# Two steps at a time in the first layer of a two-layer graph attention kernel: scores of both in a run, products of both in a run, the large unit behind

## The chip, the cores and the metric

The kernel runs on one core of one Trainium2 chip. A core has TensorE (matrix products, results into PSUM), VectorE, ScalarE and GpSimd (called POOL in the profile) for the rest, and SyncE (SP), which here only issues DMAs. Each engine takes its instructions strictly in the order in which the program issues them, and an instruction that waits holds up all that stand behind it on that engine. The metric is the device time of one execution, in microseconds, as the median of several runs.

## The reference

The input is 16 graphs of 1024 nodes with 256 features each, and a 0/1 adjacency matrix of 1024 x 1024 for each graph. Two layers follow one another. Each normalises its input, cuts it off at zero, and adds masked attention over the neighbours to the input. The first has 4 heads of 64, the second 8 heads of 32 with biases for q, k and v:

```python
h = jnp.maximum(_layernorm(x, axis=-1), 0.0)
x = x + _L0_gnn_ref(h, adj, Wq, Wk, Wv, Wo, bo)     # 4 heads of 64
h = jnp.maximum(_layernorm(x, axis=-1), 0.0)
x = x + _L1_gnn_ref(h, adj, Wq, bq, Wk, bk, Wv, bv, Wo, bo)   # 8 heads of 32

# inside a layer
scores = jnp.einsum('bhne,bhme->bhnm', Q, K) * scale
scores = jnp.where(mask, scores, -jnp.inf)
attn = jax.nn.softmax(scores, axis=-1)
heads = jnp.einsum('bhnm,bhme->bhne', attn, V)
out = concat(heads) @ Wo.T + bo
```

All of it is in fp32.

## The kernel before

The attention of the whole batch is one list of 768 **steps**. A step covers 512 queries (a half of the graph's rows) and four blocks of 128 keys x 512 queries. In layer 0 these are two heads times two key blocks, in layer 1 four heads times one key block. A **group** is the steps of one half and one set of heads: 4 steps in layer 0, 8 in layer 1. So a layer of one graph is 4 groups: 16 steps in layer 0, 32 in layer 1. The list starts with layer 0 of the first two graphs (32 steps), and then layer 1 of graph b and layer 0 of graph b+2 alternate, to the end.

For each step the program issues:

- **scores** (L447): four products of keys and queries into two PSUM buffers of the tag `ps_s`. There are three such buffers in all, each of two banks; the large units below use them too.
- **exponentials** (L463, L469): for each of the two buffers VectorE puts the mask on the scores, from PSUM into the SBUF tile p, and ScalarE takes the exponential in place. VectorE's L463 is what makes a score buffer free again.
- **weigh** (L481): the products with V, two steps later (`LEAD` is 2), into the PSUM tile po of the group, of which there is one.

The softmax's sums are column sums of p. In layer 0, `add_tiles` adds up a group's tiles (L490 on VectorE, L493 on POOL or VectorE, L494 and L496 on POOL), and `count_added` sums the result over the keys by a product with ones (L343). In layer 1 POOL adds pairs of tiles (L582), a DMA that accumulates adds those into one another (L568, issued by POOL), and `count` (L343) does the rest.

When a group has ended, a chain of small units follows at set distances, each entered in a table of due times by `later(i + k, f)` in `end_group` (L611): `copy_out` (L354, ScalarE, at once: it frees po), `spread` (ScalarE copy L362, then DMAs on SP that lay the sums over the partitions, L375, tile `sums`), `invert` (a reciprocal on VectorE, L383, and a DMA, L385), `fetch` (DMAs on SP, L393), `normalize` (POOL, L399), and for every second group `end_half`: the output product (L429), VectorE's addition to x (L434), and in layer 1 the DMAs to the output (L437).

Other due entries prepare coming layers: statistics (L191 to L201), normalisation (L210), turning of the normalised rows through DMAs (L236, L241, L248), the projections k, q (L266) and v (L302) with their copies out of PSUM (k: L274 or L280 on ScalarE; q: L272 or L278 on VectorE; v: L306 on ScalarE), bias (L219, POOL), the loading of x (L135, SP), the adjacency (L148, issued by POOL), its transpose by DMA (L154, SP) and its change into masks (L163, L171, ScalarE), and `test` (L288, VectorE), which checks the range of the sums.

The units `k`, `q`, `values` and `end_half` are called **large** (L25): they are long products on TensorE, each through one of the three score buffers. Within one step's due entries they are issued last (`rank`, L523). On an even step with a large unit the products with V are put off to the next step:

```python
if i % 2 or not self.large(i):
    for st in waiting:
        weigh(st)
```

So TensorE's order is "scores, products" step by step, or over two steps "scores, large unit, scores, products of two steps". All is issued by hand in this order (`manual_schedule`); the order of issue is the order of each queue.

In a layer-0 stage of 16 steps that begins at step a, the large units stand at a (k of layer 1), a+2 (q), a+4 (output of the layer-1 half before), a+8 (v) and a+12 (output of the other half).

Of the kernel before, what the change touches and what calls it, by code (L numbers as in the profile page):

```python
# [22 lines left out]
LEAD = 2  # L23
# [65 lines left out]
def fast_program(ctx, tc, a, w, loads, chk):  # L89
# [24 lines left out]
    def psum_pair(name):  # L114
        return ps_s.tile([P, 2, 512], F32, tag="ps_s", name=name)
# [323 lines left out]
    def scores(st):  # L439
        gr = st.gr  # L440
        D = gr.D
        st.ps = [psum_pair(f"ps_{st.n}_{i}") for i in range(2)]
        st.blocks = []
        for i in range(4):
            r, kt = (i, st.j) if gr.layer else (i % 2, 2 * st.j + i // 2)
            st.blocks.append((r, kt))
            nc.tensor.matmul(  # L447
                st.ps[i // 2][:, i % 2, :],
                gr.inp.kT[r * D : (r + 1) * D, gr.g, ts(kt, P)],
                gr.inp.qT[gr.qh][r * D : (r + 1) * D, gr.g, :],  # L450
                start=True, stop=True,
            )

    def exponentials(st, between):


        gr = st.gr
        odd = st.j % 2
        st.p = pp.tile([P, 4, 512], F32, tag=f"p{odd}", bufs=2 if odd else 7, name=f"p_{st.n}")
        for i in range(2):  # L460
            half = st.p[:, ts(i, 2), :]
            kt = st.blocks[2 * i][1]
            nc.vector.scalar_tensor_tensor(  # L463
                out=half,
                in0=gr.mask.m[gr.qh][:, kt, :].unsqueeze(1).to_broadcast([P, 2, 512]),
                scalar=-EDGE if gr.layer else BIG, in1=st.ps[i],
                op0=ALU.add if gr.layer else ALU.mult, op1=ALU.min,
            )
            nc.scalar.activation(half, half, AF.Exp, scale=gr.scale)  # L469
            if i == 0:  # L470
                for f in between:
                    f()

    def weigh(st):
        gr = st.gr
        D = gr.D
        if st.j == 0:
            gr.o = ps_o.tile([P, 512], F32, tag="po", name=f"po_{gr.n}")
        for i, (r, kt) in enumerate(st.blocks):
            h = gr.g * gr.per + r  # L480
            nc.tensor.matmul(  # L481
                gr.o[r * D : (r + 1) * D, :], gr.inp.v[:, kt, h * D : (h + 1) * D],
                st.p[:, i, :], start=(kt == 0), stop=(kt == NT - 1),
            )

    def add_tiles(one, two):


        a, b = one.p[:, 0:2, :], one.p[:, 2:4, :]
        nc.vector.tensor_add(a, a, b)  # L490

        engine = nc.vector if one.j else nc.gpsimd
        engine.tensor_add(b, two.p[:, 0:2, :], two.p[:, 2:4, :])  # L493
        nc.gpsimd.tensor_add(a, a, b)  # L494
        if one.j:
            nc.gpsimd.tensor_add(a, a, one.gr.t)  # L496
        one.gr.t = a

    def layer_steps(inp, mask):
        steps = []  # L500
        for qh in range(QH):
            half = Step()
            for g in range(2):
                steps += Group(inp, mask, qh, g, half).steps()
        return steps

    class Stream:
# [19 lines left out]
        def run(self):  # L527
            steps = self.steps
            n = len(steps)
            waiting = []  # L530
            for i in range(n + LEAD):
                now = steps[i] if i < n else None
                if i >= LEAD:
                    waiting.append(steps[i - LEAD])
                if now:
                    scores(now)
                copies = []
                if i % 2 or not self.large(i):
                    for st in waiting:
                        weigh(st)  # L540
                    for st in waiting:
                        if st.gr.layer:
                            self.count_steps(i, st)
                        if st.last:
                            copies.append(st.gr.copy_out)
                            self.end_group(i, st.gr)
                    waiting = []
                due = self.due.pop(i, [])

                for f, args in due:  # L550
                    if f.__name__ in COUNTS:
                        f(*args)
                if now:
                    exponentials(now, copies)
                else:
                    for f in copies:
                        f()
                if i % 2 and 3 <= i <= n and steps[i - 2].gr.layer == 0:
                    add_tiles(steps[i - 3], steps[i - 2])
                for f, args in sorted(due, key=self.rank):  # L560
                    if f.__name__ not in COUNTS:
                        f(*args)
            while self.due:
                for f, args in self.due.pop(min(self.due)):
                    f(*args)
# [140 lines left out]
    steps = layer_steps(inputs[0][0], masks[0])  # L706
# [37 lines left out]
    for t in range(NT):  # L744
        i = 5 + 2 * t
# [8 lines left out]
    for b in range(B - 1):  # L754
# [32 lines left out]
        else:  # L787
            last, e = inputs[1][b + 1], c + 32
# [256 lines left out]
```

## Time and profile before

| what | before |
|---|---|
| median of 3 runs | 3203.17 us (3202.34 to 3205.19) |
| the profiled execution | 3201.31 us |
| its span, first to last instruction | 3199.5 us |
| granted TensorE clock, mean | 0.997 |
| busy: TensorE / VectorE / ScalarE / POOL | 99% / 79% / 70% / 74% |
| layer-0 stage, 1113.76 to 1192.89 us | 79.13 us: TensorE 79.13, VectorE 63.99, ScalarE 51.06, POOL 53.28 busy |
| layer-1 stage, 1192.89 to 1309.13 us | 116.24 us: TensorE 115.91, VectorE 95.09, ScalarE 88.33, POOL 94.69 busy |
| opening 32 layer-0 steps, 37.90 to 206.76 us | 168.86 us: TensorE 165.86 busy |

A line of the timeline gives the start in us, the duration, the engine, the line of the kernel, the operation with its tiles and shapes, and how many records were merged. TensorE's fp32 products have two records each: x8 is one step's four products, x16 two steps'. Ends of products are modelled, so lengths are better read from one start to the next. A line of waits gives who waited for whom, the total in us, how often, and the longest. `[x <-who]` behind a timeline line is idle time of that engine just before it, and who ended it. SP and the queues of DMAs are listed as issues: the transfer ends later.

### The profile page before, as it was taken

Reading aid. Unit: us, or ns where it says so; the run is one execution under the profiler, and the core shown is the slowest. Engines: PE = TensorE matmul, PEld = TensorE weight load, DVE = VectorE, ACT = ScalarE, POOL = GpSimd, SP = SyncE. Lnnn points to the kernel's source line nnn. Section 1 sums busy time; section 2 is a strip of 40 time slices with the busy share of each in tenths; the row PEclk is TensorE's granted clock in tenths of the full one; section 3 lists DMA queues with packets and bytes.
Section 4 is the critical chain, followed back from the end, with each engine's and each line's share of the span. In section 5 each row is a group of like instructions: output and inputs, shape, how many; then the busy total and the mean of one; then the engine's idle time right before and its main releaser. Section 6 shows DMA issues by size and latency. Waiting matters only on the chain.

```text
span 3199.5 us, 44432 instructions
## 1 busy us (share of the span) xinstructions
PE 3153.7 (99%) x16662; PEld 1212.4 (38%) x16662; DVE 2532.5 (79%) x2786; ACT 2242.4 (70%) x2472; POOL 2352.4 (74%) x1103
## 2 busy tenths in 40 slices
PE   8999999999999999999999999999999999999998
PEld 3443433433334333333433334343343333333332
DVE  5677787887878888787887878878788887887776
ACT  5667677776767767677676776767777676775765
POOL 4567677786877868678686776877778687786776
PEclk9999999999999999999999999999999999999999
DMA  6326556364563645646465463655636456462321
GB/s 132 53 47 131 108 112 130 88 135 106 111 134 92 130 104 109 131 99 129 95 127 117 101 134 92 131 104 112 135 88 133 108 111 135 91 131 62 85 62 32
DMA packets 347792, 341.21 MB, mean 107 GB/s; under 512 B 196016, under 2 KB 290480, under 8 KB 330544
## 3 DMA queue, kind: packets, MB, share of 16 engines
q0 software_dynamic: 37584, 173.03, 29.2%
q1 hardware_dynamic: 309984, 165.26, 21.5%
q8 instruction: 133, 2.18, 0.3%
q14 instruction: 91, 0.75, 0.1%
HBM read 149.95 MB, written 47.96 MB: 62 GB/s over the span
## 4 chain that ended last, share of the span: by engine, by line
PE 89%; ACT 4%; DVE 3%; POOL 2%; issue 1%; DMA 1%; SPq 0%; DVEq 0%; POOLq 0%; ACTq 0%
PE ps L447 31%; PE po L481 27%; PE pq L266 13%; PE py L429 7%; PE pv L302 6%; PE pz L343 5%; DVE p L463 2%; ACT p L469 2%; ACT hn L210 1%; ACT mask L163 1%; POOL p L582 1%; POOL rstd L199 0%; ACT v L306 0%; DVE st L191 0%; DMA hT<-turned 0%
## 5 line engine op out<-in xcount | busy, mean ns | idle before, releaser
L463 DVE SCALAR_TENSOR_TENSOR p<-mask,ps 128x1024 f32<-128x1024 fp8e5 x1536 | 1796.8, 1212 | 461.3 <-PE ps L447 423.6
L469 ACT ACTIVATE p<-p 128x1024 f32<-128x1024 f32 x1536 | 1609.4, 1056 | 784.9 <-DVE p L463 745.4
L582 POOL TENSOR_TENSOR p<-p,p 128x2048 f32<-128x2048 f32 x255 | 1171.3, 4596 | 250.0 <-PE po L481 152.3
L447 PE MATMUL ps<-qT,kT 32*128 32x512 f32 (+1 forms) x6144 | 1134.1, 631 | 7.2 <-ACT v L306 4.4
L481 PE MATMUL po<-p,v 128*32 128x512 f32 (+1 forms) x6144 | 990.6, 601 | 2.1 <-ACT cat L354 1.8
L447 PEld LDWEIGHTS ps<-qT,kT 32*128 32x128 f32 (+1 forms) x6144 | 363.7, 184 | 706.2 <-issue 308.6
L494 POOL TENSOR_TENSOR p<-p 128x1024 f32<-128x1024 f32 x128 | 301.9, 2358 | 284.0 <-DVE p L493 275.3
L481 PEld LDWEIGHTS po<-p,v 128*32 128x32 f32 (+1 forms) x6144 | 229.2, 118 | 690.8 <-issue 500.3
L493 POOL TENSOR_TENSOR p<-p 128x1024 f32<-128x1024 f32 x64 | 150.8, 2357 | 173.3 <-DVE p L490 101.5
L266 PE MATMUL pq<-hT,wk 128*128 128x512 f32 x512 | 242.8, 618 | 8.9 <-DMA hT<-turned 6.3
L302 PE MATMUL pv<-wv,hT 128*128 128x256 f32 x1024 | 237.8, 385 | 0.0
L266 PE MATMUL pq<-hT,wq 128*128 128x512 f32 x512 | 236.6, 605 | 0.0
L429 PE MATMUL py<-wo,cat 128*128 128x256 f32 x1008 | 235.5, 386 | 0.5 <-POOL cat L399 0.2
L302 PEld LDWEIGHTS pv<-wv,hT 128*128 128x128 f32 x1024 | 189.4, 190 | 70.5 <-DVE p L463 30.4
L429 PEld LDWEIGHTS py<-wo,cat 128*128 128x128 f32 x1008 | 185.6, 190 | 72.5 <-issue 31.4
L343 PE MATMUL pz<-p,ones 128*32 128x512 f32 (+1 forms) x1248 | 196.1, 595 | 0.8 <-ACT s L362 0.8
L399 POOL TENSOR_TENSOR cat<-cat,inv 128x512 f32<-128x512 f32 x127 | 185.4, 1460 | 5.0 <-DMA inv<-vd 3.1
L219 POOL TENSOR_TENSOR x<-x,bo 128x1024 f32<-128x1024 f32 x64 | 152.1, 2376 | 15.8 <-DMA bo<-in_bo_dram 15.8
L490 DVE TENSOR_TENSOR p<-p 128x1024 f32<-128x1024 f32 x128 | 163.2, 1275 | 0.0
L210 ACT ACTIVATE hn<-x,shift,rstd 128x256 f32<-128x256 f32 x256 | 138.2, 588 | 24.9 <-DMA turned<-hn 17.7
L496 POOL TENSOR_TENSOR p<-p,p 128x1024 f32<-128x1024 f32 x64 | 151.5, 2367 | 5.0
L266 PEld LDWEIGHTS pq<-hT,wk 128*128 128x128 f32 x512 | 94.4, 194 | 153.3 <-issue 112.9
(51 smaller groups left out, 1665.4 us busy)
## 6 DMA issues: line engine op xcount, KB each, us to landing
p<-p POOLq DMA_DIRECT2D x133, 1024.0 KB, 7.7
adj<-in_adj_dram POOLq DMA_DIRECT2D x128, 256.0 KB, 4.2
turned<-hn SPq DMA_DIRECT2D x58, 512.0 KB, 2.9
hT<-turned SPq DMA_DIRECT2D x232, 128.0 KB, 3.1
x<-in_x_dram SPq DMA_DIRECT2D x128, 128.0 KB, 2.7
inv<-vd SPq DMA_DIRECT2D x128, 128.0 KB, 2.9
inv<-vd SPq DMA_DIRECT2D x252, 64.0 KB, 3.6
out_dram<-x SPq DMA_DIRECT2D x124, 128.0 KB, 2.4
```

The lines of the kernel that those rows point to most:

```text
L210: nc.scalar.activation(hn[:, ts(i, E)] if whole else self.blocks(half)[:, :, i, :], rows if whole else rows.rearrange("p (c q) -> p c q", ...
L266: nc.tensor.matmul(pq[:, m, :], wt[self.layer][:, c, ts(m, P)], self.hT[half][:, c, :], start=(c == 0), stop=(c == 1),)
L302: nc.tensor.matmul(pv[:, i, :], self.hT[half][:, c, ts(i, P)], w.v[self.layer][:, c, :], start=(c == 0), stop=(c == 1),)
L343: nc.tensor.matmul(self.s[r * self.D : (r + 1) * self.D, :], w.ones.to_broadcast([P, self.D]), p[:, r, :], start=start, stop=stop,)
L399: nc.gpsimd.tensor_mul(o, o, self.inv)
L429: nc.tensor.matmul(py[:, i, :], self.half.cat[:, c, ts(i, P)], w.o[self.layer][:, c, :], start=(c == 0), stop=(c == 1),)
L447: nc.tensor.matmul(st.ps[i // 2][:, i % 2, :], gr.inp.kT[r * D : (r + 1) * D, gr.g, ts(kt, P)], gr.inp.qT[gr.qh][r * D : (r + 1) * D, gr.g ...
L463: nc.vector.scalar_tensor_tensor(out=half, in0=gr.mask.m[gr.qh][:, kt, :].unsqueeze(1).to_broadcast([P, 2, 512]), scalar=-EDGE if gr.layer ...
L469: nc.scalar.activation(half, half, AF.Exp, scale=gr.scale)
L481: nc.tensor.matmul(gr.o[r * D : (r + 1) * D, :], gr.inp.v[:, kt, h * D : (h + 1) * D], st.p[:, i, :], start=(kt == 0), stop=(kt == NT - 1),)
L494: nc.gpsimd.tensor_add(a, a, b)
L582: nc.gpsimd.tensor_add(one, one, st.p)
```

## The change

The loop over steps takes two steps at once where the first belongs to layer 0, and one as before where it belongs to layer 1. For a pair (i, i+1) of layer 0 the order of issue is now: the scores of both steps; the products with V of steps i-2 and i-1, without putting off; sums that are due at i or i+1; the exponentials of both steps, with the copy of a finished group behind the first half of the first; `add_tiles`; and then the due entries of i and after them those of i+1, each set with its large units last. No due time is changed, and no instruction is added or left out; only the order differs. Since the layer-0 stages begin at even steps, the pairs are (a, a+1), (a+2, a+3) and so on.

```diff
-            waiting = []
-            for i in range(n + LEAD):
-                now = steps[i] if i < n else None
-                if i >= LEAD:
-                    waiting.append(steps[i - LEAD])
-                if now:
-                    scores(now)
+            waiting, i = [], 0
+            while i < n + LEAD:
+                wide = 2 if i < n and steps[i].gr.layer == 0 else 1
+                span = range(i, i + wide)
+                now = [steps[k] for k in span if k < n]
+                waiting += [(k, steps[k - LEAD]) for k in span if k >= LEAD]
+                for st in now:
+                    scores(st)
                 copies = []
-                if i % 2 or not self.large(i):
-                    for st in waiting:
+                if wide == 2 or i % 2 or not self.large(i):
+                    for _, st in waiting:
                         weigh(st)
-                    for st in waiting:
+                    for k, st in waiting:
                         if st.gr.layer:
-                            self.count_steps(i, st)
+                            self.count_steps(k, st)
                         if st.last:
                             copies.append(st.gr.copy_out)
-                            self.end_group(i, st.gr)
+                            self.end_group(k, st.gr)
                     waiting = []
-                due = self.due.pop(i, [])
+                due = [e for k in span for e in sorted(self.due.pop(k, []), key=self.rank)]
 
                 for f, args in due:
                     if f.__name__ in COUNTS:
                         f(*args)
-                if now:
-                    exponentials(now, copies)
-                else:
-                    for f in copies:
-                        f()
-                if i % 2 and 3 <= i <= n and steps[i - 2].gr.layer == 0:
-                    add_tiles(steps[i - 3], steps[i - 2])
-                for f, args in sorted(due, key=self.rank):
+                for st in now:
+                    exponentials(st, copies)
+                    copies = []
+                for f in copies:
+                    f()
+                for k in span:
+                    if k % 2 and 3 <= k <= n and steps[k - 2].gr.layer == 0:
+                        add_tiles(steps[k - 3], steps[k - 2])
+                for f, args in due:
                     if f.__name__ not in COUNTS:
                         f(*args)
+                i += wide
```

## The prediction

> **What bounds the kernel now.** I read the page first: its busy shares, then the chain that ended last.
>
> ```profile
> PE 3153.7 (99%) x16662; PEld 1212.4 (38%) x16662; DVE 2532.5 (79%) x2786; ACT 2242.4 (70%) x2472; POOL 2352.4 (74%) x1103
> PE 89%; ACT 4%; DVE 3%; POOL 2%; issue 1%; DMA 1%; SPq 0%; DVEq 0%; POOLq 0%; ACTq 0%
> ```
>
> TensorE is busy in 99% of the span and is 89% of the chain. The list of TensorE's waits holds 39 us in all, mostly at the two ends; in the middle it waits for nobody:
>
> ```profile
> PE ps L447 <- DVE p L463: 0.9, 4, 0.3
> PE pz L343 <- ACT s L362: 0.8, 1, 0.8
> ```
>
> So anything that shortens TensorE's stream shortens the span, and any wait put in front of it lengthens the span one for one. Next the timeline of one layer-0 stage of 16 steps, 1113.76 to 1192.89 (79.13 us). There are 14 such stages after the opening 32 layer-0 steps. TensorE, then the other queues:
>
> ```profile
> 1130.55 3.65 PE L481 MATMUL po<-p,v 128*64 128x512 f32 x16
> 1134.13 1.99 PE L447 MATMUL ps<-qT,kT 64*128 64x512 f32 x8
> 1136.05 3.72 PE L429 MATMUL py<-wo,cat 128*128 128x256 f32 x16
> 1139.70 1.99 PE L447 MATMUL ps<-qT,kT 64*128 64x512 f32 x8
> ...
> 1148.11 1.94 PE L481 MATMUL po<-p,v 128*64 128x512 f32 x8
> 1149.98 1.99 PE L447 MATMUL ps<-qT,kT 64*128 64x512 f32 x8
> ```
> ```profile
> 1128.20 0.83 POOL L568 DMA_DIRECT2D p<-p  x1
> 1133.78 2.34 POOL L493 TENSOR_TENSOR p<-p 128x1024 f32<-128x1024 f32 x1 [4.75 <-DVE p L490]
> 1136.20 2.37 POOL L494 TENSOR_TENSOR p<-p 128x1024 f32<-128x1024 f32 x1
> ```
> ```profile
> 1141.06 1.85 SPq L437 DMA_DIRECT2D out_dram<-x  x4
> 1145.03 1.75 SPq L135 DMA_DIRECT2D x<-in_x_dram  x4
> 1146.83 1.28 SPq L154 DMA_TRANSPOSE adjT<-adj  x1
> 1148.15 2.55 SPq L375 DMA_DIRECT2D sums<-s  x4
> ```
>
> A step's products alone take 1149.98 - 1148.11 = 1.87, two steps' in a run 1134.13 - 1130.55 = 3.58, so a turn out of the products costs 2 x 1.87 - 3.58 = 0.15. A step's scores take 1.92 to the next start; their four rounds are 0.43 apart in the trace, so a turn out of the scores costs about 0.20. A large unit with the turn behind it takes 3.63 to 3.65.
>
> **The gain.** Call the stage's steps a to a+15 and the pairs p0 to p7. The large units stand at a (K), a+2 (Q), a+4 (output), a+8 (V), a+12 (output). Their five pairs ran scores, unit, scores, products of two steps; now scores of two steps, products, unit: one turn out of scores fewer, 0.20 each. The three other pairs lose a turn of each kind, 0.35. Together 5 x 0.20 + 3 x 0.35 = 2.05 us a stage; by the same count about 4 in the opening.
>
> **PSUM.** There are three score buffers, and a run of two steps wants four: its last waits until the first mask operation (L463) has ended. With VectorE free that starts 1.18 after the run and takes 1.21, done at 2.44 with 0.05 to the wake-up; the last quarter is due at 2.68. So VectorE may come 0.23 late at no cost. Anything later stalls TensorE one for one plus 0.1. Before, products or a unit stood between, and the trace has L463 starting up to 2 to 3 us late (1152.97 against 1149.98) with no stall. This cover goes.
>
> I followed all queues through one stage with the durations of its rows. Most lateness is covered: VectorE's 4 x 1.13 for masks plus 1.2 or 2.5 of additions fits in a pair of 7.22; L288's waits behind POOL fall under a longer wait below; the Q copy and the output's addition end at 1.4 and 1.25 after the run's start. Five places aren't covered.
>
> (1) **p0, 0.55.** The copy of the finished group (L354) stands on ScalarE behind the first exponential and now waits for products at 5.6 after the pair's start. Three exponentials (0.96 apart), the mask step (1.04) and K's copies (1.3) follow, ending at 11.35; K's buffer is due at 9.12 + 1.82 = 10.94. Ends: 0 if ScalarE overlaps better, 0.9 if not.
>
> (2) **p2, 2.55.** The accumulating DMA L568 due at a+2 now stands on POOL behind the additions L493 and L494 of that pair, which wait for VectorE. With p1's products at time 0: L490 ends at 2.8, L493, L494 and L399 take 2.36 + 2.36 + 1.27 with their gaps, L568 is issued at 9.1 and lands 7.7 later (6.9 to 9.9 over all) at 16.8. The count that reads it (L343, due a+5) comes at 3.58 + 3.63 + 3.64 + 3.48 = 14.33. Ends 1.7 and 4.7; before, 17 us lay between issue and count.
>
> (3) **p4, 4.0.** SP works in order: after the output's addition of a+4 it issues output, x, transpose and then `sums`. By the rows above the last `sums` lands 12.2 after that addition began (1139.81, to 1150.12 + 1.9). The reciprocal L383 due at a+7 reads them. Before, from unit's end to reciprocal were 16.7 us (1139.70 to 1156.37). Now the unit ends directly at p3, which has no unit and lasts 7.22; VectorE reaches the reciprocal about 7.2 into it and is held until 12.3. Behind it stand p4's masks. The first starts at 12.5, 5.3 after p4's start instead of at most 1.41: 3.9 plus 0.1. Ends 3.5 and 4.5.
>
> (4) **p6, 2.1.** The mask load L148 of a+8 is now behind POOL's additions: issued 1.6 after p5's start. From L148 to `sums` landed were 8.8 (1162.60 to 1169.52 + 1.9; the transpose stands between). So the reciprocal of a+11 runs at 10.4, and p6's first mask 3.4 after its start. Ends 1.5 and 2.7.
>
> (5) **Start of layer 1, 3.3.** As (3), with the output of a+12 and the reciprocal of a+15: `sums` landed 13.65 after the addition here (1180.45 to 1192.21 + 1.9), so the first layer-1 mask starts 11 to 14 after p7's start; the second score step behind K, due at 11.9, waits for two masks. Ends 1.8 and 4.1.
>
> **Moved at no cost.** POOL: L399 of a+2, a+7 and a+10 follow the additions too, but the output units that read them come 5.8, 25 and 4 us after; L148 of a+4 lands by 3 into p3 and its transpose is needed in p4; L219 has only later layers waiting. ScalarE: the normalisation of a+13 waits for L199 and L201, now behind two additions, and pushes p7's exponentials back by some 4 us; their products follow only at a+17, 13 us after the scores. SP: place (L248) and fetch (L393) slip by up to 10 us behind `sums`, and their readers stand a stage and a pair later. Without these covers each would cost what it slips. p's buffers: the tightest, the odd step's second one, is free 0.4 before its mask.
>
> **The clock.** After TensorE's idle times of 4.13 and 2.17 us the granted clock was 0.51, and K took longer than its 3.70:
>
> ```profile
> 249.33 5.95 PE L266 MATMUL pq<-hT,wk 128*128 128x512 f32 x8 [4.13 <-DMA hT<-turned]
> ```
> ```profile
> 3008.49 4.93 PE L266 MATMUL pq<-hT,wk 128*128 128x512 f32 x7 [2.17 <-DMA hT<-turned]
> ```
> ```profile
> 3008.40:3011.80 3.40, 3.31 (x4) 1.51 (x5) 2.29 (x7) 2.99 (x3) 2.55 (x3) 0.51 0.38 77
> ```
>
> 3.4 us at half speed cost 1.7. Waits (2) to (5) are of this size, but a slow stretch after (3) only eats into (4). I take 1.0 a stage, ends 0 and 3.4, as not every gap need do it. The Trainium skill ("TensorE: Matmul & The Clock Gate", section "HAM oscillation — how this bites in real kernels") asks only that no gap exceed about 3.4 us. By that rule only (3) would slow the clock, (4) would take it up, and the sum would be 13 lower; the row with 2.17 speaks against so lenient a reading.
>
> **Sum.** A standard stage: -2.05 + 0.55 + 2.55 + 4.0 + 2.1 + 3.3 + 1.0 = +11.45; 13 of them (the ones that load x and masks for a later element): +149. The last layer-0 stage has no such loads: -2.05 + 0.55 + 2.55 + 0.3 = +1. The opening: -4, plus some 2 for a transpose that now waits for normalisation behind four exponentials, plus three groups with (4)'s wait: about +4. Together +154. The profiled execution ran 3201.31 (span 3199.5, 1.8 outside) and the median of three is 3203.17; I add to the median: about 3357.
>
> **Rivals.** *The turns saved and nothing else*: 14 x 2.05 + 4 = 33 off, 3170. For it: TensorE waits for nobody now, and all engines but it are at 70 to 79%. It decides where the waits add up to less than 2.05 a stage; against it, (3) alone is 4.0, with a slack of 16.7 needed 12.2. *Only (1) and (2) come true*, the sums landing in time: -2.05 + 0.55 + 2.55 = +1.05 a stage, 3217. For it: the reciprocal's waits for `sums` add up to only 7.5 us now; against it, one of those (0.41 before 1194.18) is the place of (5), so it has no slack even today. *The clock as the new bound*: each gap of 2 us or more halves it and nothing absorbs it: up to 18 a stage with all upper ends, 3420 to 3440. *It cancels out*: gain and waits within 0.2%, if pairs with units hide (3) and (5).
>
> **How the numbers follow.** The five waits with the turns: 0.72, its own range 3295 to 3415 (all lower ends together give 6.5 a stage, 3288; all upper ends are the clock rival). Only (1) and (2): 0.11. Turns alone: 0.07. Clock: 0.07. Cancelling: 0.03. The range goes down to 3212, which takes in the second rival, and up to 3415. A measurement of this kernel tells about 0.2%, 6.4 us; faster 0.07, same 0.03, slower 0.90.
>
> **What the profile after would show.** The gain: TensorE's timeline with L447 x16 and L481 x16, 3.64 and 3.58 to the next start. (2): TensorE's L343 waiting for the DMA p<-p some 14 times by about 2.5. (3) to (5): VectorE's L383 waiting for `sums`, 7.5 us grown to 100 to 170, and TensorE's L447 waiting for L463, 0.9 grown to some 120. (1): L447 waiting for the K copy L280 by about half a microsecond. Clock: granted TensorE clock below 0.99. The prediction is wrong if layer-0 stages come out at 77 us and TensorE's list of waits stays short; it is wrong in its parts if TensorE waits for ScalarE or the key projections instead.

## The result and the profile after

The change makes the kernel slower: 3395.99 us (3375.64 to 3401.86) against 3203.28 us (3202.34 to 3205.19). The ratio is 1.059, with a 95% interval of 1.0543 to 1.0636. The profile below is of an execution of 3401.86 us, with a span of 3400.0 and a mean granted clock of 0.974. In it the lines after L565 have moved down by three: the accumulating DMA is L571, and POOL's addition of layer 1 is L585.

The page of the kernel after, its busy shares and the chain that ended last:

```profile
PE 3224.3 (95%) x16662; PEld 1246.3 (37%) x16662; DVE 2495.0 (73%) x2786; ACT 2215.5 (65%) x2472; POOL 2349.9 (69%) x1103
PE 64%; ACT 10%; DVE 8%; DMA 6%; POOL 5%; issue 4%; SPq 2%; DVEq 0%; ACTq 0%; POOLq 0%
```

TensorE has fallen from 89% of the chain to 64%. No single engine took its place; what it lost is spread over ScalarE, VectorE, DMAs and POOL. Its busy time grew by 71 us although it runs the same 16662 products: that is mostly work at half clock. From the mean clocks, (1 - 0.974) x 3400 = 88 us are lost now and (1 - 0.997) x 3199.5 = 10 were lost before, so the clock alone accounts for some 78 of the 200 us (an estimate from the two means).

The list of waits, TensorE's first, then one line of VectorE's and one of ScalarE's (total us, how often, longest):

```profile
PE ps L447 <- DVE p L463: 83.5, 39, 4.9
PE pz L343 <- DMA p<-p: 34.0, 14, 3.5
PE py L429 <- POOL cat L399: 5.4, 11, 0.5
PE ps L447 <- ACT kT L280: 3.5, 15, 0.8
```
```profile
DVE vn L383 <- DMA sums<-s: 150.4, 33, 6.3
```
```profile
ACT cat L354 <- PE py L429: 313.6, 30, 13.6
```

The first two were 0.9 us and absent before, and the reciprocal's wait for the sums grew from 7.5 us to 150.4. The last line is new and large, and the prediction did not have it.

Stage by stage, each from its first scores to those of the next (mean over the 13 layer-0 stages of the middle, the layer-1 stage after each, and the time in each for which the granted clock was 0.5, called half clock here):

| | before | after | half clock, after |
|---|---|---|---|
| opening | 168.85 | 184.50 | 10.2 |
| layer-0 stage | 79.14 | 87.44 | 5.78 |
| layer-1 stage | 116.12 | 121.64 | 5.78 |
| last layer-0 stage | 79.4 | 84.0 | 3.4 |

13 x (8.30 + 5.52) + 15.65 + 4.6 = 199.9 of the 200.5 us by which the span grew. Of a round's 13.8 us (one stage of each layer), TensorE's idle times grew by 8.6 and half of 11.55 us at half clock is 5.78; with the gain of 2.05 off, 12.3. The other 1.5 show when TensorE's runs are read from one start to the next, against the kernel with every queue mended (at the end of the experiments). In the round below, five runs of layer 0 are longer by 0.07 to 0.27 us each than their idle time and the clock explain, and the stalled score step of layer 1 by some 0.8: the second half of its scores waited for L463 once more, which shows in the weight loads alone, since the modelled ends of the first half cover it (`PEld` is TensorE's weight load):

```profile
1067.59 0.50 PEld L447 LDWEIGHTS ps<-qT,kT 32*128 32x128 f32 x4 [0.83 <-DVE p L463]
```

One layer-0 stage of TensorE's timeline, 973.55 to 1059.73 (86.18 us), with what follows; the rows between are left out where nothing waits:

```profile
973.55 3.70 PE L447 MATMUL ps<-qT,kT 64*128 64x512 f32 x16
...
984.85 1.99 PE L447 MATMUL ps<-qT,kT 64*128 64x512 f32 x8 [0.20 <-ACT kT L280]
986.77 3.65 PE L481 MATMUL po<-p,v 128*64 128x512 f32 x16
990.36 3.70 PE L266 MATMUL pq<-hT,wq 128*128 128x512 f32 x8
993.99 3.83 PE L447 MATMUL ps<-qT,kT 64*128 64x512 f32 x16
...
1003.70 1.06 PE L343 MATMUL pz<-p,ones 128*32 128x512 f32 x8 [2.30 <-DMA p<-p]
...
1021.93 1.52 PE L447 MATMUL ps<-qT,kT 64*128 64x512 f32 x4 [3.52 <-DVE p L463]
1023.38 4.91 PE L481 MATMUL po<-p,v 128*64 128x512 f32 x16
...
1049.22 3.29 PE L429 MATMUL py<-wo,cat 128*128 128x256 f32 x14 [0.49 <-POOL cat L399]
...
1066.46 3.21 PE L447 MATMUL ps<-qT,kT 32*128 32x512 f32 x8 [1.96 <-DVE p L463]
1069.59 5.70 PE L481 MATMUL po<-p,v 128*64 128x512 f32 x16
```

The runs x16 are there: 3.63 to 3.64 us for two steps' scores to the next start, 3.59 for two steps' products. So are the waits, one after another. The two products of 4.91 and 5.70 us are 3.65 us elsewhere; they are what a slow clock costs. Windows of the same stage (start and end, then the busy times of five engines, the granted clock, DMA share and GB/s):

```profile
1003.70:1007.10 3.40, 3.40 (x19) 2.30 (x20) 0.00 (x0) 0.00 (x0) 3.32 (x2) 1.00 0.02 5
1021.93:1025.30 3.37, 3.37 (x10) 0.99 (x12) 3.33 (x3) 1.04 (x1) 1.92 (x2) 0.59 0.32 85
1066.46:1071.50 5.04, 5.04 (x14) 1.47 (x16) 4.94 (x8) 3.70 (x5) 1.61 (x1) 0.55 0.41 156
```

After the gap of 2.30 us the clock stayed full. After those of 3.52 and 1.96 it halved, and after the shorter of the two for longer; the last section says what goes with it.

Why the longest wait is there is read from SP's queue and VectorE's, of the kernel after:

```profile
1009.71 2.04 SPq L437 DMA_DIRECT2D out_dram<-x  x4
1013.68 1.75 SPq L135 DMA_DIRECT2D x<-in_x_dram  x4
1015.48 1.28 SPq L154 DMA_TRANSPOSE adjT<-adj  x1
1016.80 2.49 SPq L375 DMA_DIRECT2D sums<-s  x4
```
```profile
1008.45 1.23 DVE L434 TENSOR_TENSOR x<-py,x 128x1024 f32<-128x1024 f32 x1 [5.94 <-PE py L429]
...
1020.54 0.25 DVE L383 RECIPROCAL vn<-sums 128x16 f32<-128x16 f32 x1 [4.88 <-DMA sums<-s]
1020.72 4.55 DVE L463 SCALAR_TENSOR_TENSOR p<-mask,ps 128x1024 f32<-128x1024 fp8e5 x4
```

`sums` is the fourth in line on SP behind output, x and transpose; the reciprocal gets it 12.1 us after the output's addition began, and the masks for which TensorE waits stand behind the reciprocal.

### The profile page after: what moved, and what is told of

Read it like the earlier page. It is cut to its first block, busy times and chain, and to the rows that moved or that the text cites. A ratio compares the mean times of both kernels' runs of the same rounds, so it can differ in the third digit from the quotient of the medians.

```text
span 3400.0 us, 44449 instructions
## 1 busy us (share of the span) xinstructions
PE 3224.3 (95%) x16662; PEld 1246.3 (37%) x16662; DVE 2495.0 (73%) x2786; ACT 2215.5 (65%) x2472; POOL 2349.9 (69%) x1103
## 4 chain that ended last, share of the span: by engine, by line
PE 64%; ACT 10%; DVE 8%; DMA 6%; POOL 5%; issue 4%; SPq 2%; DVEq 0%; ACTq 0%; POOLq 0%
PE ps L447 20%; PE po L481 18%; PE pq L266 9%; PE py L429 7%; DVE p L463 6%; ACT p L469 6%; PE pv L302 5%; PE pz L343 5%; DMA p<-p 3%; DMA sums<-s 2%; POOL p L493 2%; ACT hn L210 1%; POOL cat L399 1%; ACT mask L163 1%; DVE p L490 1%
## 5 line engine op out<-in xcount | busy, mean ns | idle before, releaser
L463 DVE SCALAR_TENSOR_TENSOR p<-mask,ps 128x1024 f32<-128x1024 fp8e5 x1536 | 1786.9, 1213 | 439.4 <-PE ps L447 401.9
L469 ACT ACTIVATE p<-p 128x1024 f32<-128x1024 f32 x1536 | 1586.9, 1055 | 619.9 <-DVE p L463 585.7
L585 POOL TENSOR_TENSOR p<-p,p 128x2048 f32<-128x2048 f32 x255 | 1174.3, 4608 | 237.3 <-PE po L481 141.6
L447 PE MATMUL ps<-qT,kT 32*128 32x512 f32 (+1 forms) x6144 | 1148.2, 638 | 94.1 <-DVE p L463 83.5
L481 PE MATMUL po<-p,v 128*32 128x512 f32 (+1 forms) x6144 | 1022.3, 615 | 2.1 <-ACT cat L354 1.8
L447 PEld LDWEIGHTS ps<-qT,kT 32*128 32x128 f32 (+1 forms) x6144 | 375.8, 185 | 783.2 <-DVE p L463 320.6
L481 PEld LDWEIGHTS po<-p,v 128*32 128x32 f32 (+1 forms) x6144 | 243.6, 121 | 728.6 <-issue 502.6
L494 POOL TENSOR_TENSOR p<-p 128x1024 f32<-128x1024 f32 x128 | 301.1, 2352 | 300.7 <-DVE p L493 295.7
L354 ACT COPY cat<-po 128x512 f32<-128x512 f32 x128 | 74.0, 578 | 480.3 <-PE py L429 313.6
L429 PE MATMUL py<-wo,cat 128*128 128x256 f32 x1008 | 246.8, 398 | 5.6 <-POOL cat L399 5.4
L343 PE MATMUL pz<-p,ones 128*32 128x512 f32 (+1 forms) x1248 | 197.2, 599 | 34.8 <-DMA p<-p 34.0
L429 PEld LDWEIGHTS py<-wo,cat 128*128 128x128 f32 x1008 | 193.1, 197 | 84.5 <-issue 32.1
L399 POOL TENSOR_TENSOR cat<-cat,inv 128x512 f32<-128x512 f32 x127 | 184.0, 1449 | 5.4 <-DMA inv<-vd 3.6
L219 POOL TENSOR_TENSOR x<-x,bo 128x1024 f32<-128x1024 f32 x64 | 155.0, 2422 | 15.7 <-DMA bo<-in_bo_dram 15.6
L434 DVE TENSOR_TENSOR x<-py,x 128x1024 f32<-128x1024 f32 x63 | 76.9, 1220 | 121.2 <-PE py L429 120.0
L571 POOL DMA_DIRECT2D p<-p x133 | 118.0, 888 | 54.5 <-POOL p L585 31.4
```

The source lines that it names most:

```text
L343: nc.tensor.matmul(self.s[r * self.D : (r + 1) * self.D, :], w.ones.to_broadcast([P, self.D]), p[:, r, :], start=start, stop=stop,)
L399: nc.gpsimd.tensor_mul(o, o, self.inv)
L429: nc.tensor.matmul(py[:, i, :], self.half.cat[:, c, ts(i, P)], w.o[self.layer][:, c, :], start=(c == 0), stop=(c == 1),)
L447: nc.tensor.matmul(st.ps[i // 2][:, i % 2, :], gr.inp.kT[r * D : (r + 1) * D, gr.g, ts(kt, P)], gr.inp.qT[gr.qh][r * D : (r + 1) * D, gr.g ...
L463: nc.vector.scalar_tensor_tensor(out=half, in0=gr.mask.m[gr.qh][:, kt, :].unsqueeze(1).to_broadcast([P, 2, 512]), scalar=-EDGE if gr.layer ...
L481: nc.tensor.matmul(gr.o[r * D : (r + 1) * D, :], gr.inp.v[:, kt, h * D : (h + 1) * D], st.p[:, i, :], start=(kt == 0), stop=(kt == NT - 1),)
```

## The experiments

The theory is that of the prediction: the two runs gain about 2 us a stage, and what the order puts behind POOL's additions and behind SP's other DMAs costs more, through TensorE's waits and then the clock. The first rival is that the runs themselves are what costs, since three score buffers are too few for them. The second is that the clock, and not the waits, takes most.

**The accumulating DMA first.** Of a pair's due entries, `accumulate` goes ahead of the exponentials and `add_tiles`:

```diff
+                if wide == 2:
+                    for f, args in due:
+                        if f.__name__ == "accumulate":
+                            f(*args)
+                    due = [e for e in due if e[0].__name__ != "accumulate"]
                 for st in now:
                     exponentials(st, copies)
```

> The changed kernel, but in a pair of layer-0 steps POOL issues the accumulating DMA before the additions of that pair and not after them. Theory of the queues (lateness on POOL, SP and VectorE that the new order makes): TensorE's wait of L343 for the DMA p<-p, 34.0 us in 14 places, falls below 3 us, everything else stays; the time falls by 25 to 45 us from 3396, to about 3360. Rival, the three score buffers (a run of two steps wants four, so the run itself is what stalls): no change, 3385 to 3405. Rival, the clock alone: no change beyond its own scatter.

It took 3385.31 us in one run, clock 0.973. That lies within the scatter of the changed kernel's own runs (3375.64 to 3401.86), so most of the expected gain is missing. The wait it was aimed at is gone: TensorE's list no longer has L343 behind the DMA p<-p. Its other lines, and VectorE's wait and the place in the stage, of this kernel:

```profile
PE ps L447 <- DVE p L463: 116.8, 38, 7.5
```
```profile
DVE vn L383 <- DMA sums<-s: 183.2, 32, 8.9
```
```profile
1020.02 2.08 PE L447 MATMUL ps<-qT,kT 64*128 64x512 f32 x4 [5.98 <-DVE p L463]
```

33 us came back on the line behind the masks. The output unit of a+4 now ends earlier, but `sums` does not come earlier by as much. SP's queue in this kernel:

```profile
1005.34 1.77 SPq L437 DMA_DIRECT2D out_dram<-x  x4
1011.73 1.75 SPq L135 DMA_DIRECT2D x<-in_x_dram  x4
```

The load of x follows the output's DMAs by 6.4 us, where it was 4.0 in the kernel after; here they are issued within 0.01 us of POOL's mask load L148 (1005.33). That the two transfers get into each other's way fits, but was not tried by itself. Shown is that TensorE waited as long as before, only further on: a wait in front of another one is worth only what the second does not take over.

**The sums first.** The DMAs that spread the sums go ahead of the other due entries of the pair, and so ahead of output, x and transpose on SP:

```diff
                 due = [e for k in span for e in sorted(self.due.pop(k, []), key=self.rank)]
+                if wide == 2:
+                    due.sort(key=lambda e: e[0].__name__ != "spread")
```

> The changed kernel, but among the due entries of a pair the spreading of the sums comes first, so that SP issues these DMAs ahead of the output's, x's and the transpose; TensorE's order is untouched. Theory of the queues: VectorE's wait of L383 for sums, 150.4 us, falls below 30; TensorE's wait of L447 for L463, 83.5 us, falls below 30; without these gaps the stretches at half clock mostly go too; per stage 3.5 + 2.0 of waits and some 4 to 5 of half clock: 110 to 150 us less, 3250 to 3285. Rival, the score buffers: L447 waits for L463 as before, because VectorE frees the fourth buffer too late by its own work; 3385 to 3405.

It took 3256.29 us in one run, clock 0.994: 140 us off by one reordering. A layer-0 stage has 80.03 us on average, a layer-1 stage 118.08, and half clock appears in only one of the 13 pairs of stages. TensorE's waits in this kernel:

```profile
PE pz L343 <- DMA p<-p: 22.3, 14, 2.9
PE ps L447 <- DVE p L463: 9.0, 10, 3.2
```
```profile
DVE vn L383 <- DMA sums<-s: 31.5, 37, 1.8
```

The reciprocal's wait for `sums`, 150.4 us in the changed kernel, is down to 31.5. So SP's order, the prediction's (3) to (5), was the bulk of the loss, together with the half clock that followed from it.

**Both first.** Both edits together.

> Both moves together; the runs of two steps and the large unit behind stay. Theory of the queues: nearly the whole loss goes: 3215 to 3245, with some waits left in the opening 32 steps (16 us there) and 0.5 a stage behind the copy of K. If the runs save 2.05 a stage as predicted, the layer-0 stages come out at 77.5 to 79.5 us. Rival, the score buffers: stages stay above 84 us, 3380 and more.

It took 3231.32 us (3227.64 to 3231.84), ratio 1.0091 (1.0074 to 1.0108). A layer-0 stage is now 78.34 us, shorter than before's 79.14, but the opening is still 182.9 and a layer-1 stage 118.00.

**The copy behind both steps' exponentials**, in addition to both edits above. L354, which copies a finished group out of PSUM, goes into one of two `cat` buffers. The output product that reads the older one is now issued behind it in the pair, so ScalarE stands still until that product is done:

```diff
                 for st in now:
-                    exponentials(st, copies)
-                    copies = []
-                for f in copies:
-                    f()
+                    exponentials(st, copies if wide == 1 else [])
+                if wide == 2 or not now:
+                    for f in copies:
+                        f()
```

> All pairs, sums and accumulation issued first as in the run of both, and in addition the copy of a finished group stands behind both steps' exponentials, not behind the first half of the first. If ScalarE, held by that copy until the output product has read its buffer, is what still lengthens the start of layer 1 (+1.3 to +2.8 us a stage) and of p0 and p6, layer 1 falls to 116.05 to 116.5 and a layer-0 stage from 78.37 to 77.1 to 77.8, and 3231 falls by 13 x (1.7 + 0.6 to 1.2) to about 3193 to 3202, with the opening still long. If POOL's additions are what lengthen it, layer 1 stays at 117.4 to 118.9 and the time at 3222 to 3232.

It took 3205.69 us (3204.32 to 3210.61), ratio 1.0015 (1.0005 to 1.0024), a little above what was expected. A layer-0 stage fell to 77.85 and the opening to 177.4; a layer-1 stage fell only to 117.35 and not to 116.1. So the copy explains 0.65 of the 1.9 us there. For the rest POOL's additions are not needed: VectorE's list of waits in this kernel has a new line,

```profile
DVE st L191 <- DMA x<-in_x_dram: 42.5, 15, 4.2
```

against 6.0 us, two times, before. With the sums put first, the load of x is what is late on SP, and the statistics that read it stand in front of masks of layer 1. One such place, VectorE's rows first and then TensorE's:

```profile
1206.30 0.43 DVE L191 BATCH_NORM_STATS2 st<-x 128x6 f32<-128x256 f32 x1 [3.31 <-DMA x<-in_x_dram]
1207.54 2.33 DVE L463 SCALAR_TENSOR_TENSOR p<-mask,ps 128x1024 f32<-128x1024 fp8e5 x2
```
```profile
1208.33 1.59 PE L447 MATMUL ps<-qT,kT 32*128 32x512 f32 x8
1213.57 2.20 PE L447 MATMUL ps<-qT,kT 32*128 32x512 f32 x8
```

Such a step of scores takes 1.14 us elsewhere. These two are 1.5 us longer together, and this stage took 117.79, 1.55 more than the same stage before; the list of TensorE's idle times holds none of it.

**Pairs only where neither step has a large unit:** three of the eight pairs, the other steps issued as before.

```diff
-                wide = 2 if i < n and steps[i].gr.layer == 0 else 1
+                pair = i < n and steps[i].gr.layer == 0 and i % 2 == 0
+                wide = 2 if pair and not (self.units(i) or self.units(i + 1)) else 1
```

> Two steps at a time only where neither step has a large unit due (three of eight pairs of a stage); the others as in the kernel before. Theory of the queues: no unit is pushed behind, so sums and the accumulating DMA are in time as before; each of the pairs loses two turns of 0.20 and 0.15: 3 x 0.35 = 1.05 a stage, some 15 us in all; 3184 to 3196. Rival, the score buffers: each run of two steps stalls by itself, three times a stage, so slower than 3203.

It took 3299.81 us (3296.38 to 3301.82), ratio 1.0306 (1.0289 to 1.0324): a clear miss. Waits of TensorE, then its timeline and POOL's around one of them, of this kernel:

```profile
PE py L429 <- POOL cat L399: 76.4, 14, 5.6
```
```profile
1004.17 0.70 PE L429 MATMUL py<-wo,cat 128*128 128x256 f32 x2
1010.48 4.80 PE L429 MATMUL py<-wo,cat 128*128 128x256 f32 x14 [5.61 <-POOL cat L399]
```
```profile
1002.13 2.35 POOL L493 TENSOR_TENSOR p<-p 128x1024 f32<-128x1024 f32 x1 [2.29 <-DVE p L490]
1004.55 2.35 POOL L494 TENSOR_TENSOR p<-p 128x1024 f32<-128x1024 f32 x1
1006.86 2.34 POOL L219 TENSOR_TENSOR x<-x,bo 128x1024 f32<-128x1024 f32 x1
1009.16 1.26 POOL L399 TENSOR_TENSOR cat<-cat,inv 128x512 f32<-128x512 f32 x1
```

The normalisation L399 of a+10 stands behind three of POOL's long additions, and the output product of a+12 needs it. It stands so in the kernel after as well, where the wait is only 0.49 us: there the output product comes behind the scores and products of the whole pair, 8.08 us after the pair's first scores (1039.95 to 1048.03), and here behind one step's scores, after 1.92 us (1002.25 to 1004.17).

**No runs.** The changed order of all other entries is kept, but each pair issues scores, products, scores, products:

```diff
-                for st in now:
-                    scores(st)
+                if wide == 2:
+                    for st in now:
+                        scores(st)
+                        if waiting:
+                            weigh(waiting[st is not now[0]][1])
+                else:
+                    for st in now:
+                        scores(st)
...
-                    for _, st in waiting:
-                        weigh(st)
+                    if wide == 1:
+                        for _, st in waiting:
+                            weigh(st)
```

> The changed kernel without its runs: in a pair TensorE gets scores, products, scores, products and then the large unit; everything else (unit behind, due entries of both steps behind both exponentials) as changed. Theory of the queues: the units' place and the grouped due entries make the loss, so it stays: the turns' gain of some 33 to 39 us is lost again, and the waits of L447 for L463 are about 2 us shorter at two places a stage, as the fourth score buffer is wanted later; 3360 to 3410, and VectorE's wait of L383 for sums stays above 100 us. Rival, the score buffers: without a run of two steps' scores nothing wants four buffers at once; 3200 to 3225.

It took 3414.16 us in one run, a little above what was expected, and VectorE's L383 waited 130.4 us for `sums`. Without the runs the loss is still there, so neither the runs nor their want of a fourth score buffer is its cause; the kernel with every queue mended, below, has all the runs and hardly a wait. The waits of TensorE:

```profile
PE pz L343 <- DMA p<-p: 52.5, 14, 4.0
PE ps L447 <- DVE p L463: 50.5, 35, 3.1
```

**Work put into the gaps.** The changed kernel with score products issued once more, 138 products of 0.43 us, 59 us in all, in front of the waits:

```diff
+            if i == 1:
+                for r, kt in st.blocks * fill(st):
+                    nc.tensor.matmul(
+                        st.ps[0][:, r % 2, :],
...
+        if gr.layer:
+            return 2 if gr.qh == 0 else 0
+        return 3 if gr.qh == 1 and gr.inp.b > 1 else 0
```

> The changed kernel with idle time of TensorE filled: ahead of the two places where it waits longest for VectorE (the fourth score buffer of steps a+8, a+9, and the second score step of layer 1) the score products just issued are repeated, 2.6 us and 1.7 us of work, about 60 us in all, with the same results into the same buffer. If the idle gaps halve the clock and that costs as much as the waits: the stretches at half clock go down from some 180 us to below 80, and the time falls by 20 to 70 us in spite of the added work, to 3325 to 3375. If the clock costs nothing to speak of: the same time or up to 15 us more.

It took 3365.82 us (3358.23 to 3372.16), ratio 1.0517 (1.05 to 1.0535): more work, and 30 us less than the changed kernel. In the profiled execution (3358.23 us, clock 0.990) half clock falls from 5.78 to 2.36 us in a layer-0 stage and from 5.78 to 0.26 in a layer-1 stage. So the clock is a cost of its own behind the waits, and the second rival holds in part.

**Pairs without large units, in the order of due times.** The entries of the pair's first step that are not large stand ahead of `add_tiles`, those of the second behind, as in the kernel before:

```diff
+                first = list(self.due.get(i, []))
...
+                rest = [e for e in due if e[0].__name__ not in COUNTS]
+                lead = [e for e in rest if e in first] if wide == 2 else []
+                for f, args in lead:
+                    f(*args)
                 for k in span:
                     if k % 2 and 3 <= k <= n and steps[k - 2].gr.layer == 0:
                         add_tiles(steps[k - 3], steps[k - 2])
-                for f, args in due:
-                    if f.__name__ not in COUNTS:
-                        f(*args)
+                for f, args in rest[len(lead):]:
+                    f(*args)
```

> Two steps at a time only where neither has a unit due, as in the run before of that kind, and in such a pair the due entries of the first step are issued ahead of the additions, as in the kernel before. Theory of the queues: the wait of the output product L429 for L399 (76.4 us in 14 places there) goes, because L399 no longer stands behind L493 and L494 on POOL; what is left are the turns, 1.05 a stage: 3180 to 3196, faster than before by 0.2 to 0.7%. If the short pairs cost something of their own, it stays above 3203.

It took 3200.53 us (3192.39 to 3203.3), ratio 0.9993 (0.9984 to 1.0002). The wait of the run above for L399 is gone, and every one of the 14 layer-0 stages took 77.95 us, 1.18 less than before where 1.05 was expected of three pairs. Of these 16.5 us in the profiled execution the opening, with 176.25 us, ate 7.4 and one layer-1 stage, with 124.08, another 7.9: there a DMA to `turned` held ScalarE's normalisation for 10.0 us.

**The same without the opening.** Its 32 steps are issued one at a time (`pair = 4 * NT <= i < n and ...`).

> The pairs in the old order of small entries (as in the run of pairs in due order), but the opening's 32 steps are issued one at a time. If the miss of the run in due order was the opening alone (176.25 us in place of 168.85) and the stages keep 77.95 us (14 x 1.18 us under 79.13), the time is 3201.5 - 14 x 1.18 = 3185 us, 3183 to 3192 with the clock's scatter. If the order of the stages is at fault (their lateness adding up, or a gap at the start of layer 1), it stays at 3196 to 3206.

It took 3184.08 us (3183.65 to 3185.29), ratio 0.9941 (0.9925 to 0.9958), with every layer-0 stage at 77.95 or 77.96 and the opening at 168.85. Between the two profiled executions lie 17.3 us: 7.4 are the opening, and 7.9 the one slow layer-1 stage, which did not come back here. So the stages keep their gain, but the opening by itself was less than half of what was missing; whether it also brings about the late DMA was not tried.

**All eight pairs, with every queue mended:** no pairs in the opening, the copy behind both exponentials, and ahead of `add_tiles` first `spread` and then the small entries of the first step.

```diff
-                wide = 2 if i < n and steps[i].gr.layer == 0 else 1
+                wide = 2 if 4 * NT <= i < n and steps[i].gr.layer == 0 else 1
...
+                if wide == 2:
+                    lead = [e for e in rest if e[0].__name__ == "spread"]
+                    lead += [e for e in rest if e in first and not self.rank(e) and e not in lead]
+                    rest = [e for e in rest if e not in lead]
```

> All layer-0 pairs from step 32 on as changed, runs and unit behind, but with the due entries mended: the spreading of the sums first, then the small entries of the first step, then the additions, then the rest; and the copy of the finished group behind both exponentials, so that it doesn't hold ScalarE until the output product behind it. The opening 32 steps one at a time. Theory of the queues: stages at 77.1 to 77.8 us, layer 1 at 116.1 to 117 us, opening 169: 3170 to 3195. If runs of two steps cost more than these orders, stages stay at 78.4 and layer 1 at 118 us: 3210 and more.

It took 3182.49 us (3181.64 to 3185.36), ratio 0.9941 (0.9926 to 0.9956), and so beats both kernels. TensorE's waits in this kernel, where the changed one had 83.5 and 34.0 us:

```profile
PE ps L447 <- DVE p L463: 1.1, 5, 0.3
```

A layer-0 stage takes 77.07 us as a rule, 2.07 less than before, and a layer-1 stage 116.05. That should put it 12 us below the run before this one, and it is only level with it: one layer-1 stage took 124.61, where a DMA to `turned` (landed after 3.5 us in the median of this kernel) held ScalarE's normalisation for 9.8 us. It is the same wait as in the run of pairs in due order; why the DMA came late in these two is open.

## Why the prediction was right

The sign and the mechanism came out, and the size roughly: 3396 was measured, 3357 predicted (193 us more than before where 154 were forecast); 3295 to 3415 was the likeliest case's own range. Point by point, in us, the stage shown above against the mended kernel's, in which TensorE runs the same order with hardly a wait:

| term | predicted | measured | by what row |
|---|---|---|---|
| gain of the turns | -2.05 | -2.07 | mended stage 77.07 against 79.14 |
| (1) key copy | 0.55 | 0.47 | 982.67 to 993.99 |
| (2) accumulating DMA | 2.55 | 2.37 | 993.99 to 1008.35, wait 2.30 |
| (3) sums behind SP's queue | 4.0 | 3.5, with the clock 5.4 | 1015.56 to 1032.73, wait 3.52 |
| (4) sums behind the mask load | 2.1 | 0.0, and 0.8 of something else | 1039.95 to 1052.44 |
| (5) start of layer 1 | 3.3 | 2.0, from start to start 2.7, with the clock 5.5 on average | wait 1.96 and what follows it |
| clock, a round | 1.0 | 5.78, part of the 5.4 and 5.5 | 11.55 us at half clock |

- **The gain** was worked out from a turn (the change from one kind of product to the next) of 0.20 and one of 0.15 us. 5 x 0.20 + 3 x 0.35 = 2.05 stands against 2.07 in the mended kernel, 3 x 0.35 = 1.05 against 1.18 in the one with three pairs. *The turns saved and nothing else* was what the order could have given, not what it gave.
- **(1), (2) and (3)** came where they were put, within 0.5 us. For (3), `sums` was expected 12.2 us after the addition began; 12.1 were measured.
- **(4) was oversized.** It rested on L148 of a+8 being issued 1.6 after p5's start. It was issued at 1032.88, 0.15 after p5's start at 1032.73, because TensorE had lost 5.4 us in the pair before while POOL had not: in the run with the copy behind both steps' exponentials, where TensorE is on time, it is issued 3.49 after p5's start. A slow stretch eats the next wait; the prediction said so of the clock, and did not apply it to POOL. In p6 a wait of 0.49 for L399 shows instead.
- **L399 of a+10 was put under "moved at no cost",** on a cover of 4 us. None of it was left: POOL's L219 (2.38 us) stood ahead of it too, L399 itself took 2.25 us, and TensorE waited 0.49. That is no effect of TensorE's lateness, as the wait is the same in the run with the copy behind both steps' exponentials, where TensorE is on time:

```profile
PE py L429 <- POOL cat L399: 6.7, 13, 0.5
```

With the output product 6.2 us earlier, as in the run of pairs without large units, the same instruction costs 5.6 us a stage.

- **The clock was the mis-sized term.** The value taken was 1.0 a stage "as not every gap need do it", with an upper end of 3.4. Each gap that halved it did so for 3.4 or 6.8 us, and there were mostly two a round; the measured 5.78 lies above the upper end. The run with work put into the gaps shows the cost by itself. On the other side (3) to (5) were put at 9.4 and came to 7.2 in this round, read from start to start with the clock's part off (3.7, 0.8 and 2.7). Some 2 us too much of waits stand against 4.8 too little of clock, so that a round came out as near as 13.8 to the 11.45 forecast is in part luck. The case *the clock as the new bound* was therefore closer to the truth than its 0.07, though its 3420 to 3440 was not reached: (4) fell away, and (5) stayed below its 3.3.
- **The opening** was given +4 and cost 15.65. Of this, 12.75 are TensorE's waits and 5.1 half clock, less some 2 for the turns. The two longest: 3.20 us for L463, behind VectorE's statistics of the next input, and 4.99 us for ScalarE's normalisation L210, which stood on ScalarE behind the group copy, the exponentials and changes of masks. I had costed the second at some 2 and not followed VectorE there. The last layer-0 stage was given +1 and cost 4.6: L343 waited 3.50 us for the accumulating DMA there, and 3.4 us of half clock followed.
- **ScalarE's wait on the `cat` buffer** (L354 behind L429, 313.6 us) was not in the prediction at all: I had followed the copy to the products it reads, not to the product that frees the buffer it writes. Putting the copy behind both exponentials took back 0.5 us of a layer-0 stage, 0.65 of a layer-1 stage and 5.5 of the opening, once the larger waits were gone.
- **The rival *Only (1) and (2) come true*** is refuted by the run that put the sums first: (3) to (5) and the clock behind them were worth 140 of the 193 us.

## What to carry to other kernels

When an order is changed, follow each queue that a moved instruction now stands behind, SP's DMAs and POOL's among them, and both ends of every buffer: who fills it and who frees it. A wait in front of another is worth only what the second does not take over: with the accumulating DMA first, 34 us went and 33 came back. A cover holds only for the order in which it was read: the same normalisation L399 cost 0.5 us with the output product late in the pair and 5.6 with it early. And where gaps of about 2 us appear in TensorE's stream, price the clock for each of them: with more than 2.1 us of a 3.41 us window idle it halved every time.

## What the runs showed of the hardware

- The clock is decided on a fixed grid of 3.413 us. In the kernel after, half clock begins at 1022.54, 1066.92 and 1213.69: 13 and 43 times 3.413 apart; all 34 beginnings in this kernel, without the first 40 and last 150 us, fit the grid within 0.01 us. What goes with it is TensorE's idle time inside one window of the grid. The gap of 2.30 us (1001.40 to 1003.70) is cut by the grid's line at 1002.06 into 0.66 and 1.64, and went free; that of 1.96 lies in one window. Over six runs (the kernel after, the accumulation first, the sums first, pairs without units, no runs, work put into the gaps) I took all windows at full clock, without the first 40 and last 150 us, with at least 0.7 us idle: over 2.1 us idle, half clock followed in 80 of 80; under 1.5 us, in 10 of some 120; the change lies at 1.7 to 1.9, about half a window. So gaps of equal length cost nothing or 1.7 or 3.4 us by where they fall, and stages of the same order came out at 86.1 or 88.8 us; the scatter of 26 us among the runs of the changed kernel fits this. Why one slow stretch lasts one window and another two is open. The Trainium skill ("TensorE: Matmul & The Clock Gate", section "HAM oscillation — how this bites in real kernels") puts its rule at gaps above about 3.4 us; the runs put it at some 1.7 to 2.1 us idle within a window of that length.
- A small instruction of VectorE with two operands in SBUF waited for a running operation of POOL. In the opening of the kernel after, `ve` of 128x4 elements took 2.27 us, ending as POOL's L494 did (start 52.55, 2.34 us); with POOL idle it takes 0.16. Of the 64 rows of L195 in that kernel 19 start beside a running POOL operation, and each ends 0.02 to 0.03 us after it. VectorE's L434, of whose operands one lies in PSUM, took 1.22 us beside POOL too:

```profile
52.64 2.27 DVE L195 TENSOR_TENSOR ve<-mv,numbers 128x4 f32<-128x4 f32 x1
```

The Trainium skill ("SBUF — State Buffer", section "SBUF: two separate sides") says that the two engines share a pair of ports under an exclusive lock for a whole instruction, and these rows agree.
